# The expert mixture of the last layer: units of four experts in place of units of two, with the banks and buffers laid out for them

## The chip, the cores and the metric

The kernel runs on one core of a Trainium2 chip. Its time is the device time of one execution in microseconds, and the figure for a kernel is the median of several executions. Five engines work in parallel, each through its own instructions in order: TensorE (PE, with its weight loads shown apart as PEld), VectorE (DVE), ScalarE (ACT), GpSimd (POOL) and SyncE (SP). They wait for one another and for DMA transfers through semaphores.

## The reference, cut to what matters

Four transformer layers run one after the other on 1024 rows of 256 numbers. The change lies in the feed-forward part of the last layer, a mixture of 64 experts of which each row uses 8, beside one shared expert:

```python
logits = h @ router_w.T
probs = softmax(logits)
top_vals, top_idx = top_k(probs, 8)
top_vals = top_vals / sum(top_vals)
for e in range(64):                     # each with 64 hidden numbers
    g, u = split(h @ gate_up_proj[e].T, 2)
    out += (silu(g) * u) @ down_proj[e].T * weight_of(row, e)
x = layernorm(x + out + sigmoid(h @ shared_gate) * shared_expert(h))
```

All numbers are float32.

## The kernel before, in words

The stage before the mixture (`attn3`) also routes: it scatters each row, together with its expert numbers, weights and places, into a table in DRAM that has a region of 1024 rows for each expert. The mixture (`ffn3`) then goes through this table in groups of two kinds. An "own" group takes the first 128 rows of each of four consecutive experts. Sixteen such groups cover the 64 experts. A "more" group takes four blocks of 64 rows each, for experts that got more than 128 rows; which experts these are is decided at run time, and ten such groups always run. Further ones run under an `If` at the end only where they are needed; in the profiled execution none ran.

The groups are sorted into one list: own 0, more 0, own 1, own 2, more 1, own 3, more 2, own 4, own 5, more 3, and so on to own 14, own 15, more 9. Each group is cut into two units, so an own unit holds two experts of 128 rows and a more unit two blocks of 64 rows side by side. Every unit goes through these steps (line numbers are those of the profile):

- `load` (per group, on SP): `xr`, the rows from the table (L2414 for own, L2427 for more), and for more groups the experts' weights `few` (L2432). Own groups 1, 3 and 5 first queue 1.5 MB of further expert weights, `gu` and `wd` (L2392, L2396).
- `turn`: PE transposes the rows (L2468), DVE copies them to `xT` (L2470).
- `find` (per group): five small DVE operations (L2446 to L2458) that give `pair`, the row's weight for this expert, and `index`, the row's place in the array of results.
- `hidden`: gate and up products on PE (L2480 own, L2493 more), Silu on ACT (L2486, L2499), and the product of the two on DVE (L2487, L2500).
- `turn_hidden`: PE transposes the hidden numbers (L2507), ACT copies them to `hT` (L2509).
- `down`: PE multiplies by the down weights (L2519, L2532), ACT scales each block of 128 rows into `y` (L2525, L2536), and POOL scatters it to `results` in DRAM with an indirect DMA (L151). An own unit has two scatters, a more unit one. All groups together have 16 x 4 + 10 x 2 = 84.

The order on every engine, SP's queue included, is the one written out by the loop in `run`, with `AHEAD = 2` groups loaded ahead:

```python
for at in range(len(units) + 2):
    if at % 2 == 0 and at // 2 + AHEAD < len(groups):
        load(groups[at // 2 + AHEAD])
    if at + 1 < len(units):
        turn(units[at + 1])
    if at < len(units):
        if at % 2 == 0:
            find(units[at][0])
        hidden(units[at])
    if 0 < at <= len(units):
        turn_hidden(units[at - 1])
    if at > 1:
        down(units[at - 2])
```

So the first `down` stands behind the fourth `turn`. A tile comes out of a pool with a fixed number of buffers; whoever first writes a buffer that is used again waits until all that read it are done, a scatter's DMA among them. The pools of this stage are listed in `SCOPES`. `y` has 5 buffers of two blocks each, and `sel` has 12 for the results of `find`. PSUM has two `wide` tiles of two banks and four single banks. After the mixture, `add_results` loads the results (L2582) when every scatter has landed, adds them up on PE (L2596) and normalises.

Of the kernel before, what the change touches and what calls it, by code (L numbers as in the profile page):

```python
# [29 lines left out]
AF = mybir.ActivationFunctionType  # L30
ALU = mybir.AluOpType
AX = mybir.AxisListType

P = 128
T = 1024
NT = T // P
D = 256
NC = D // P
HALF = 512
# [2243 lines left out]
def shared_expert(k, gate_up, down):  # L2283


    nc = k.nc
    g, u = k.bank(), k.bank()
    for j, ps in enumerate((g, u)):
        for c in range(NC):
            for half in range(2):  # L2290
                nc.tensor.matmul(
                    ps[64 * half : 64 * half + 64, :],
                    lhsT=gate_up[:, c, 64 * j : 64 * j + 64],
                    rhs=k.xcols(c, half * HALF, HALF), start=c == 0, stop=c == NC - 1,
                )
    h = k.tile("shared", [P, HALF])
    nc.scalar.activation(h, g, AF.Silu)
    nc.vector.tensor_tensor(h, h, u, ALU.mult)
    for t in range(4):
        ys = k.wide()  # L2300
        for half in range(2):
            rows = slice(64 * half, 64 * half + 64)
            nc.tensor.matmul(
                ys[:, half * HALF : half * HALF + D], lhsT=h[rows, t * P : (t + 1) * P],
                rhs=down[rows, :], start=True, stop=True,
            )
        for half in range(2):
            at = 4 * half + t
            nc.vector.scalar_tensor_tensor(
                k.x[:, at, :], ys[:, half * HALF : half * HALF + D], k.gate[:, at : at + 1],  # L2310
                k.x[:, at, :], ALU.mult, ALU.add,
            )
# [60 lines left out]
def ffn3(k, a):  # L2373
# [5 lines left out]
    nc = k.nc  # L2379
    shared = k.weights([P, NC, P], a["L3_ffn_shared_gate_up"].rearrange("(c p) f -> p c f", p=P))  # L2380
# [6 lines left out]
    gu = k.tile("gu", [P, 32, 2, NC, P])  # L2387
    wd = k.tile("wd", [P, 32, D])
# [15 lines left out]
    views = dram_disjoint_views(results, E3 + MOST)  # L2404
    regions = k.table.rearrange("(e r) w -> e r w", r=REGION)
    rows, few, xTs, hs, found = {}, {}, {}, {}, {}

    def load(group):
        kind, g = group
        xr = rows[group] = k.tile("xr", [P, 4, ROW])  # L2410
        if kind == "own":
            if g in (1, 3, 5):
                weights_for(20 + 2 * (g - 1))
            nc.sync.dma_start(  # L2414
                out=xr, in_=regions[4 * g : 4 * g + 4, :P, :].rearrange("e p w -> p e w")
            )
            return
        for i in range(2):
            q = 2 * g + i
            _, at = nc.values_load_multi_w_load_instructions(  # L2420
                where[:, q, :], engines=[mybir.EngineType.SP], min_val=0,
                max_val=E3 * REGION - 64,
                skip_runtime_bounds_check_because="both are clamped where they are made",
            )
            few[q] = k.tile("w", [P, 2, 384])
            for h in range(2):
                nc.sync.dma_start(  # L2427
                    out=xr[64 * h : 64 * h + 64, i, :], in_=k.table[bass.ds(at[h], 64), :]
                )
            for h in range(2):  # L2430
                e = at[2 + h].with_bounds(min_val=0, max_val=E3 - 1)
                nc.sync.dma_start(  # L2432
                    out=few[q][:, h, :], in_=a["L3_ffn_few"][:, bass.ds(e * 384, 384)]
                )
# [24 lines left out]
        found[group] = index, pair  # L2459

    def turn(unit):
        (kind, g), i = unit
        n = 2 if kind == "own" else 1
        xr = rows[kind, g][:, n * i : n * i + n, :]
        ps = k.bank()[:, : NC * n * P].rearrange("p (c h n) -> p c h n", c=NC, h=n)
        for c in range(NC):
            for h in range(n):
                nc.tensor.transpose(ps[:, c, h, :], xr[:, h, c * P : (c + 1) * P], k.ident)  # L2468
        xTs[unit] = k.tile("xT", [P, NC, 2, P])
        nc.vector.tensor_copy(xTs[unit][:, :, :n, :], ps)  # L2470

    def hidden(unit):
        (kind, g), i = unit
        xT, ps = xTs.pop(unit), k.bank()
        h = hs[unit] = k.tile("h", [P, 2, 64])
        if kind == "own":
            ps = ps[:, : 2 * P].rearrange("p (h n) -> p h n", h=2)
            for e in range(2):
                for c in range(NC):
                    nc.tensor.matmul(  # L2480
                        ps[:, e, :], lhsT=xT[:, c, e, :], rhs=gu[:, 2 * g + i, e, c, :],
                        start=c == 0, stop=c == NC - 1,
                    )
            gate, up = ps[:, :, :64], ps[:, :, 64:]
            s = k.tile("s", [P, 2, 64])
            nc.scalar.activation(s, gate, AF.Silu)  # L2486
            nc.vector.tensor_tensor(h, s, up, ALU.mult)  # L2487
            return
        ps = ps[:, :P]
        for c in range(NC):  # L2490
            for e in range(2):
                half = slice(64 * e, 64 * e + 64)
                nc.tensor.matmul(  # L2493
                    ps[half, :], lhsT=xT[:, c, 0, half],
                    rhs=few[2 * g + i][:, e, c * P : (c + 1) * P],
                    start=c == 0, stop=c == NC - 1,
                )
        s = k.tile("s", [P, 2, 64])[:, 0, :]
        nc.scalar.activation(s, ps[:, :64], AF.Silu)  # L2499
        nc.vector.tensor_tensor(  # L2500
            h, s.unsqueeze(1).to_broadcast([P, 2, 64]),
            ps[:, 64:].unsqueeze(1).to_broadcast([P, 2, 64]), ALU.mult,
        )

    def turn_hidden(unit):
        ps = k.bank()[:, :P]
        nc.tensor.transpose(ps, hs[unit].rearrange("p h n -> p (h n)"), k.ident)  # L2507
        hs[unit] = k.tile("hT", [P, P])
        nc.scalar.copy(hs[unit], ps)  # L2509

    def down(unit):
        (kind, g), i = unit
        hT, ys, yt = hs.pop(unit), k.wide(), k.tile("y", [P, 2, D])
        index, pair = found[kind, g]
        halves = [slice(64 * h, 64 * h + 64) for h in range(2)]
        ys = ys.rearrange("p (r n) -> p r n", r=2)
        if kind == "own":
            for h, half in enumerate(halves):
                nc.tensor.matmul(  # L2519
                    ys[:, h, :D], lhsT=hT[half, :], rhs=wd[half, 2 * g + i, :],  # L2520
                    start=True, stop=True,
                )
            for h in range(2):
                at = 2 * i + h
                nc.scalar.activation(  # L2525
                    yt[:, h, :], ys[:, h, :D], AF.Copy, scale=pair[:, at, 1:2]
                )
                k.scatter(views, index[:, at : at + 1], yt[:, h, :])
            return
        for r, part in enumerate(halves):  # L2530
            for h, half in enumerate(halves):
                nc.tensor.matmul(  # L2532
                    ys[half, r, :P], lhsT=hT[part, half],
                    rhs=few[2 * g + i][part, h, 2 * P :], start=True, stop=True,
                )
        nc.scalar.activation(  # L2536
            yt[:, 0, :].rearrange("p (r n) -> p r n", r=2), ys[:, :, :P], AF.Copy,
            scale=pair[:, i, 1:2],
        )
        k.scatter(views, index[:, i : i + 1], yt[:, 0, :])  # L2540

    AHEAD = 2

    def run(groups):
        units = [(group, i) for group in groups for i in range(2)]
        for group in groups[:AHEAD]:
            load(group)
        turn(units[0])
        for at in range(len(units) + 2):
            if at % 2 == 0 and at // 2 + AHEAD < len(groups):  # L2550
                load(groups[at // 2 + AHEAD])
            if at + 1 < len(units):
                turn(units[at + 1])
            if at < len(units):
                if at % 2 == 0:
                    find(units[at][0])
                hidden(units[at])
            if 0 < at <= len(units):
                turn_hidden(units[at - 1])
            if at > 1:  # L2560
                down(units[at - 2])

    with k.in_order(transfers=True):
        shared_expert(k, shared, shared_down)
        where, keys, longest = more_blocks(k, ids, column)
        own = [((g + 0.5) / 16, ("own", g)) for g in range(16)]
# [8 lines left out]
def add_results(k, a):  # L2575
# [39 lines left out]
    attn2: dict(wide=3, q=4, k=4, v=2, pt=3, ot=6, tops=2, parts=6),  # L2615
    ffn2: dict(p4=3, t2=8, zero=1),
    attn3: dict(q=12, k=4, v=8, pt=2, p4=2, turned=2, ot=3, t2=4, raw=2),
    ffn3: dict(gu=1, wd=1, route=14, shared=1, xr=4, xT=2, sel=12, s=2, h=2, hT=3, y=5),
    add_results: dict(r=8, z=4),
}  # L2620

# [103 lines left out]
```

## Time and profile before

| | |
|---|---|
| median of 10 executions | 2102.87 us (2098.31 to 2109.95) |
| the profiled execution | 2096.13 us, of which the span is 2094.4 us |
| mean granted TensorE clock | 0.952 |
| busy share of the span | PE 88%, PEld 56%, DVE 64%, ACT 41%, POOL 34% |
| first transposition of the mixture (L2468) | 1932.74 us |
| first and last scatter start (L151, results) | 1941.47 and 2056.83 us |
| scatters | 84, of 0.96 us each on POOL |
| first load of results (L2582) | 2060.60 us |

All times on the profile's axis count from the start of the span. In the list of groups, PE shows two records for one float32 matmul and one for a transposition, so eight records of L2480 are four matmuls. A row of the timeline gives start, duration, engine, line, operation, what is written from what, how many instructions are merged, and in brackets the engine's idle time before it with what ended it.

### The profile page before, as it was taken

The numbers are of one execution on the slowest core, as the hardware profiler recorded it, in microseconds if no ns is written. First come the engines' busy times: TensorE is split into PE (matmuls) and PEld (weight loads), VectorE is DVE, ScalarE is ACT, GpSimd is POOL, SyncE is SP. The second block draws the span as 40 slices with busy tenths as digits, with TensorE's granted clock in tenths as the row PEclk, the third lists the DMA queues.
The fourth block names the chain that finished last, engine by engine and source line by source line (L and its number), as shares of the span: only waits on it lengthen the run. The fifth ranks groups of instructions, "written<-read, shape, count | busy, mean of one in ns | idle before, by whom it ended". The sixth has DMA issues, their size and how long they took to land. (4 is left out here: it accounts for less than half of the span.)

```text
span 2094.4 us, 26185 instructions
## 1 busy us (share of the span) xinstructions
PE 1841.8 (88%) x8163; PEld 1162.8 (56%) x8163; DVE 1332.7 (64%) x2903; ACT 866.8 (41%) x2354; POOL 703.7 (34%) x942
## 2 busy tenths in 40 slices
PE   7988769699999999898889899999999877785896
PEld 4655545456676666576444444445665655554675
DVE  6788846577876665545577354445867676774463
ACT  3666614445253343434444522256444433321451
POOL 5343321333343332231111211115333253533573
PEclk9999979899999999998999999999999999887898
DMA  6322354244444643301330299922443232437985
GB/s 184 85 62 71 82 161 128 80 123 122 132 126 107 175 121 91 82 11 61 93 101 2 101 420 421 422 114 70 98 127 93 66 93 58 122 90 246 333 283 216
DMA packets 180257, 291.91 MB, mean 139 GB/s; under 512 B 36592, under 2 KB 140400, under 8 KB 170896
## 3 DMA queue, kind: packets, MB, share of 16 engines
q1 hardware_dynamic: 153056, 170.46, 29.0%
q0 software_dynamic: 25904, 118.65, 15.0%
q8 instruction: 68, 1.11, 0.2%
q10 hardware_dynamic: 1152, 1.05, 0.1%
q14 instruction: 77, 0.63, 0.1%
HBM read 96.76 MB, written 110.76 MB: 99 GB/s over the span
## 5 line engine op out<-in xcount | busy, mean ns | idle before, releaser
L174 PE MATMUL bank<-xT,w 128*128 128x512 f32 (+1 forms) x960 | 390.1, 546 | 3.9 <-DVE xT L200 2.7
L282 POOL TENSOR_SCALAR p<-p,st 128x128 f32<-128x128 f32 (+7 forms) x256 | 191.7, 749 | 495.3 <-DVE st L281 490.6
L386 DVE STREAM_TRANSPOSE turned<-p 128x128 f32<-128x128 f32 (+7 forms) x232 | 283.5, 1222 | 90.7 <-DMA pt<-turned 48.4
L423 PE MATMUL bank<-pt,v 128*128 128x256 f32 x1216 | 295.1, 388 | 28.2 <-DMA pt<-turned 27.0
L289 PE MATMUL wide<-k,q 128*128 128x512 f32 (+3 forms) x768 | 295.9, 495 | 17.4 <-ACT p L274 16.5
L423 PEld LDWEIGHTS bank<-pt,v 128*128 128x128 f32 x1216 | 237.6, 200 | 85.6 <-issue 37.9
L174 PEld LDWEIGHTS bank<-xT,w 128*128 128x128 f32 x960 | 183.6, 196 | 148.5 <-issue 129.1
L269 DVE TENSOR_REDUCE st<-wide 128x1 f32<-128x128 f32 (+7 forms) x256 | 193.3, 755 | 52.8 <-PE wide L294 46.1
L289 PEld LDWEIGHTS wide<-k,q 128*128 128x128 f32 x768 | 141.0, 192 | 132.0 <-issue 91.0
L274 ACT ACTIVATE p<-wide,st,factor 128x256 f32<-128x256 f32 (+7 forms) x128 | 106.4, 832 | 240.4 <-DVE st L271 129.3
L274 ACT ACTIVATE p<-wide,st 128x128 f32<-128x128 f32 (+7 forms) x128 | 94.9, 741 | 238.9 <-DVE st L269 217.8
L181 PE MATMUL bank<-w,xT 128*128 128x512 f32 (+2 forms) x288 | 115.9, 537 | 5.6 <-DVE xT L2004 4.1
L800 ACT ACTIVATE e<-wide,st 128x128 f32<-128x128 f32 x256 | 90.0, 377 | 73.7 <-DVE st L808 65.0
L264 DVE TENSOR_TENSOR wide<-wide,causal 128x128 f32<-128x128 f32 x192 | 55.9, 291 | 90.1 <-PE wide L289 88.6
L1675 ACT ACTIVATE pt<-wide 128x1024 f32<-128x1024 f32 (+3 forms) x96 | 75.7, 811 | 67.2 <-PE wide L1669 65.4
L151 POOL DMA_INDIRECT results<-y,sel x84 | 80.8, 962 | 52.8 <-ACT y L2525 31.9
L1678 POOL TENSOR_SCALAR_AFFINE_SELECT pt<-pt 128x256 f32<-128x256 f32 x64 | 26.0, 408 | 179.6 <-ACT pt L1675 179.2
L181 PEld LDWEIGHTS bank<-w,xT 128*128 128x128 f32 x288 | 51.7, 193 | 49.3 <-issue 37.3
L1367 POOL DMA_DIRECT2D table<-zero x64 | 34.3, 537 | 132.2 <-DMA table<-zero 132.2
L151 POOL DMA_INDIRECT table<-w x64 | 64.6, 1009 | 36.1 <-issue 14.6
L1627 DVE TENSOR_REDUCE st<-wide 128x2 f32<-128x1024 f32 x64 | 64.3, 1019 | 18.2 <-PE wide L1616 8.9
L866 PE MATMUL bank<-w,ot 128*128 128x256 f32 x256 | 63.7, 394 | 8.2 <-ACT ot L860 5.7
(393 smaller groups left out, 3269.1 us busy)
## 6 DMA issues: line engine op xcount, KB each, us to landing
table<-zero POOLq DMA_DIRECT2D x64, 1120.0 KB
pt<-turned SPq DMA_DIRECT2D x60, 240.0 KB
pt<-turned SPq DMA_DIRECT2D x60, 176.0 KB
pt<-turned SPq DMA_DIRECT2D x156, 64.0 KB
xr<-table SPq DMA_DIRECT2D x16, 560.0 KB
gu<-in_L_ffn_gate_up_dram SPq DMA_DIRECT2D x16, 512.0 KB
r<-results SPq DMA_DIRECT2D x8, 1024.0 KB
w<-in_L_ffn_few_dram SPq DMA_DIRECT2D x40, 192.0 KB
```

The source lines that it names most:

```text
L151: self.nc.gpsimd.indirect_dma_start(out=views.pop(), out_offset=bass.IndirectOffsetOnAxis(ap=index, axis=0), in_=source, in_offset=None,)
L174: self.nc.tensor.matmul(out, lhsT=weight(c), rhs=self.xcols(c, lo, n), start=c == 0, stop=c == NC - 1)
L181: self.nc.tensor.matmul(out, lhsT=self.xcols(c, lo, n), rhs=weight(c), start=c == 0, stop=c == NC - 1)
L269: nc.vector.tensor_reduce(top, scores[:, :n], axis=AX.X, op=ALU.max, negate=True)
L274: nc.scalar.activation(probs[:, :n], scores[:, :n], AF.Exp, bias=top, scale=1.0 if scale is None else scale, accum_out=total,)
L282: self.nc.gpsimd.tensor_scalar(probs[:, :n], probs[:, :n], total, 1.0, ALU.mult, ALU.mult)
L289: self.nc.tensor.matmul(s[:, lo : lo + m], lhsT=query, rhs=key(lo, m), start=True, stop=not masked or lo + m < n, skip_group_check=masked,)
L386: k.nc.vector.transpose(squares.rearrange("p b (k q) -> p b k q", q=32), probs[:, :n].rearrange("p (k i b) -> p b k i", b=4, i=32),)
L423: self.k.nc.tensor.matmul(out.rearrange("p (a q) -> p a q", q=32) if first else out.rearrange("p (s a q) -> p s a q", s=2, q=32), lhsT=val ...
L800: nc.scalar.activation(e[:, r, f, b, :], sc[:, r, f, b, :], AF.Exp, bias=top[:, at : at + 1], accum_out=total[:, at : at + 1],)
L1627: nc.vector.tensor_reduce(st[:, i, :] if half else to, sc[:, :, :n], axis=AX.X, op=ALU.max, negate=True,)
L1675: nc.scalar.activation(two[:, :, lo:], sc[:, :, lo:], AF.Exp)
```

## The change

A unit becomes a whole group: four experts, or two register pairs (four blocks of 64 rows). `turn` writes eight transpositions (four for a more unit) into one `wide` tile and copies it in two instructions. `hidden` computes all four blocks into one bank, followed by one Silu and one product. `turn_hidden` makes two transpositions into one bank and one copy. `down` keeps its matmuls, its scaling and its scatters: four of each of the last two for an own unit, two for a more unit. `AHEAD` becomes 3 and counts units. PSUM gets three `wide` tiles and two single banks. The pools change too, among them `y` to 2 buffers of four blocks and `sel` to 15. The shared expert's hidden tile moves into the pool `y`.

```diff
     def turn(unit):
-        (kind, g), i = unit
-        n = 2 if kind == "own" else 1
-        xr = rows[kind, g][:, n * i : n * i + n, :]
-        ps = k.bank()[:, : NC * n * P].rearrange("p (c h n) -> p c h n", c=NC, h=n)
+        kind, g = unit
+        xr, ps = rows[unit], k.wide()
+        n = 4 if kind == "own" else 2
+        ps = ps[:, : NC * n * P].rearrange("p (c h n) -> p c h n", c=NC, h=n)
         for c in range(NC):
             for h in range(n):
                 nc.tensor.transpose(ps[:, c, h, :], xr[:, h, c * P : (c + 1) * P], k.ident)
-        xTs[unit] = k.tile("xT", [P, NC, 2, P])
-        nc.vector.tensor_copy(xTs[unit][:, :, :n, :], ps)
+        xTs[unit] = k.tile("xT", [P, NC, 4, P])
+        for c in range(NC):
+            nc.vector.tensor_copy(xTs[unit][:, c, :n, :], ps[:, c])
...
     def hidden(unit):
-            ps = ps[:, : 2 * P].rearrange("p (h n) -> p h n", h=2)
-            for e in range(2):
+            ps = ps.rearrange("p (h n) -> p h n", h=4)
+            for e in range(4):
...
     def turn_hidden(unit):
-        ps = k.bank()[:, :P]
-        nc.tensor.transpose(ps, hs[unit].rearrange("p h n -> p (h n)"), k.ident)
-        hs[unit] = k.tile("hT", [P, P])
+        ps, h = k.bank()[:, : 2 * P], hs[unit]
+        for i in range(2):
+            nc.tensor.transpose(
+                ps[:, i * P : (i + 1) * P], h[:, 2 * i : 2 * i + 2, :].rearrange("p h n -> p (h n)"),
+                k.ident,
+            )
+        hs[unit] = k.tile("hT", [P, 2 * P])
         nc.scalar.copy(hs[unit], ps)
...
     def down(unit):
-        hT, ys, yt = hs.pop(unit), k.wide(), k.tile("y", [P, 2, D])
+        hT, ys, yt = hs.pop(unit), k.wide(), k.tile("y", [P, 4, D])
...
+            for i in range(2):
+                for h in range(2):
+                    at = 2 * i + h
+                    nc.scalar.activation(
+                        yt[:, at, :], ys[:, h, i, :], AF.Copy, scale=pair[:, at, 1:2]
+                    )
+                    k.scatter(views, index[:, at : at + 1], yt[:, at, :])
...
-    AHEAD = 2
+    AHEAD = 3
...
-            if at % 2 == 0 and at // 2 + AHEAD < len(groups):
-                load(groups[at // 2 + AHEAD])
+            if at + AHEAD < len(units):
+                load(units[at + AHEAD])
             if at + 1 < len(units):
                 turn(units[at + 1])
             if at < len(units):
-                if at % 2 == 0:
-                    find(units[at][0])
+                find(units[at])
                 hidden(units[at])
...
-    ffn3: dict(gu=1, wd=1, route=14, shared=1, xr=4, xT=2, sel=12, s=2, h=2, hT=3, y=5),
+    ffn3: dict(wide=3, gu=1, wd=1, route=10, xr=4, xT=2, sel=15, s=1, h=2, hT=2, y=2),
```

More of the change, by code (lines that the diff above doesn't have):

```diff
@@ L2295, in shared_expert @@
                 )
-    h = k.tile("shared", [P, HALF])
+    h = k.tile("y", [P, HALF])
     nc.scalar.activation(h, g, AF.Silu)
@@ L2468, in turn @@
                 nc.tensor.transpose(ps[:, c, h, :], xr[:, h, c * P : (c + 1) * P], k.ident)
-        xTs[unit] = k.tile("xT", [P, NC, 2, P])
-        nc.vector.tensor_copy(xTs[unit][:, :, :n, :], ps)
+        xTs[unit] = k.tile("xT", [P, NC, 4, P])
+        for c in range(NC):
+            nc.vector.tensor_copy(xTs[unit][:, c, :n, :], ps[:, c])
     def hidden(unit):
-        (kind, g), i = unit
+        kind, g = unit
         xT, ps = xTs.pop(unit), k.bank()
-        h = hs[unit] = k.tile("h", [P, 2, 64])
+        h = hs[unit] = k.tile("h", [P, 4, 64])
+        s = k.tile("s", [P, 4, 64])
         if kind == "own":
-            ps = ps[:, : 2 * P].rearrange("p (h n) -> p h n", h=2)
-            for e in range(2):
+            ps = ps.rearrange("p (h n) -> p h n", h=4)
+            for e in range(4):
                 for c in range(NC):
                     nc.tensor.matmul(
-                        ps[:, e, :], lhsT=xT[:, c, e, :], rhs=gu[:, 2 * g + i, e, c, :],
+                        ps[:, e, :], lhsT=xT[:, c, e, :],
+                        rhs=gu[:, 2 * g + e // 2, e % 2, c, :],
                         start=c == 0, stop=c == NC - 1,
@@ L2484, in hidden @@
             gate, up = ps[:, :, :64], ps[:, :, 64:]
-            s = k.tile("s", [P, 2, 64])
             nc.scalar.activation(s, gate, AF.Silu)
@@ L2488, in hidden @@
             return
[L2489 to L2499, printed above, removed]
+        ps = ps[:, : 2 * P].rearrange("p (i n) -> p i n", i=2)
@@ new lines, in hidden @@
+        for i in range(2):
+            for c in range(NC):
+                for e in range(2):
+                    half = slice(64 * e, 64 * e + 64)
+                    nc.tensor.matmul(
+                        ps[half, i, :], lhsT=xT[:, c, i, half],
+                        rhs=few[2 * g + i][:, e, c * P : (c + 1) * P],
+                        start=c == 0, stop=c == NC - 1,
+                    )
+        s = s[:, :2, :]
+        nc.scalar.activation(s, ps[:, :, :64], AF.Silu)
+        both = h.rearrange("p (i r) n -> p i r n", i=2)
@@ L2500, in hidden @@
         nc.vector.tensor_tensor(
-            h, s.unsqueeze(1).to_broadcast([P, 2, 64]),
-            ps[:, 64:].unsqueeze(1).to_broadcast([P, 2, 64]), ALU.mult,
+            both, s.unsqueeze(2).to_broadcast([P, 2, 2, 64]),
+            ps[:, :, 64:].unsqueeze(2).to_broadcast([P, 2, 2, 64]), ALU.mult,
         )
     def turn_hidden(unit):
-        ps = k.bank()[:, :P]
-        nc.tensor.transpose(ps, hs[unit].rearrange("p h n -> p (h n)"), k.ident)
-        hs[unit] = k.tile("hT", [P, P])
+        ps, h = k.bank()[:, : 2 * P], hs[unit]
@@ L2509, in turn_hidden @@
+        for i in range(2):
[4 more added lines that the diff above has]
+        hs[unit] = k.tile("hT", [P, 2 * P])
         nc.scalar.copy(hs[unit], ps)
     def down(unit):
-        (kind, g), i = unit
-        hT, ys, yt = hs.pop(unit), k.wide(), k.tile("y", [P, 2, D])
-        index, pair = found[kind, g]
+        kind, g = unit
+        hT, ys, yt = hs.pop(unit), k.wide(), k.tile("y", [P, 4, D])
@@ L2515, in down @@
+        index, pair = found[unit]
         halves = [slice(64 * h, 64 * h + 64) for h in range(2)]
-        ys = ys.rearrange("p (r n) -> p r n", r=2)
         if kind == "own":
[L2518 to L2528, printed above, removed]
-            return
@@ L2530, in down @@
[L2530 to L2540, printed above, removed]
@@ L2542, in ffn3 @@
-    AHEAD = 2
[L2544 to L2547, printed above, removed]
+            ys = ys.rearrange("p (r i n) -> p r i n", r=2, i=2)
+            for i in range(2):
+                for h, half in enumerate(halves):
+                    nc.tensor.matmul(
+                        ys[:, h, i, :], lhsT=hT[half, i * P : (i + 1) * P],
+                        rhs=wd[half, 2 * g + i, :], start=True, stop=True,
+                    )
@@ new lines, in down @@
+            for i in range(2):
+                for h in range(2):
+                    at = 2 * i + h
+                    nc.scalar.activation(
+                        yt[:, at, :], ys[:, h, i, :], AF.Copy, scale=pair[:, at, 1:2]
+                    )
+                    k.scatter(views, index[:, at : at + 1], yt[:, at, :])
+            return
+        ys = ys.rearrange("p (r i n) -> p r i n", r=2, i=4)
+        for i in range(2):
+            for r, part in enumerate(halves):
+                for h, half in enumerate(halves):
+                    nc.tensor.matmul(
+                        ys[half, r, i, :], lhsT=hT[part, i * P + 64 * h : i * P + 64 * h + 64],
+                        rhs=few[2 * g + i][part, h, 2 * P :], start=True, stop=True,
+                    )
+            nc.scalar.activation(
+                yt[:, i, :].rearrange("p (r n) -> p r n", r=2), ys[:, :, i, :], AF.Copy,
+                scale=pair[:, i, 1:2],
+            )
+            k.scatter(views, index[:, i : i + 1], yt[:, i, :])
@@ L2548, in run @@
+    AHEAD = 3
+    def run(units):
+        for unit in units[:AHEAD]:
+            load(unit)
         turn(units[0])
         for at in range(len(units) + 2):
-            if at % 2 == 0 and at // 2 + AHEAD < len(groups):
-                load(groups[at // 2 + AHEAD])
+            if at + AHEAD < len(units):
+                load(units[at + AHEAD])
             if at + 1 < len(units):
```

## The prediction

> **What bounds the kernel now.** I read first the chain that ended last, near its end. A row gives start, duration and what the time went to.
>
> ```profile
> 2047.03 0.66 PE wide L2519 x4
> 2047.71 0.26 ACT y L2525
> ...
> 2055.57 0.96 POOL results L151
> 2056.53 0.30 issue
> 2056.83 3.43 DMA results<-y,sel
> 2060.60 4.80 DMA r<-results
> 2065.45 23.35 PE bank L2596 x100
> ```
>
> From 1952 to 2047 this chain is PE throughout, so it looks as if PE set the pace. But it ends with a row of scatters, and nothing of the next stage can load before the last of them has landed. So I read the timeline of POOL (start, busy time, idle time before) next, and then the end of PE's.
>
> ```profile
> 1941.47 0.96 POOL L151 DMA_INDIRECT results<-y,sel  x1 [17.27 <-ACT y L2525]
> 1942.73 0.96 POOL L151 DMA_INDIRECT results<-y,sel  x1 [0.30 <-issue]
> 1950.62 0.96 POOL L151 DMA_INDIRECT results<-y,sel  x1 [6.93 <-ACT y L2525]
> ...
> 1958.05 0.96 POOL L151 DMA_INDIRECT results<-y,sel  x1 [1.25 <-ACT y L2525]
> 1959.31 0.96 POOL L151 DMA_INDIRECT results<-y,sel  x1 [0.30 <-ACT hT L2509]
> ...
> 1977.35 0.96 POOL L151 DMA_INDIRECT results<-y,sel  x1 [0.62 <-ACT y L2536]
> 1979.55 0.96 POOL L151 DMA_INDIRECT results<-y,sel  x1 [1.24 <-ACT y L2525]
> ...
> 2050.51 0.96 POOL L151 DMA_INDIRECT results<-y,sel  x1 [0.30 <-issue]
> ```
>
> ```profile
> 2048.75 0.45 PE L2532 MATMUL wide<-w,hT 64*64 64x128 f32 x8 [0.46 <-ACT hT L2509]
> ```
>
> A scatter costs 0.96 us, and 0.30 us lie before each, whatever the row names as the cause. From 1958.05 (the seventh) to 2056.83 (the last) are 77 steps in 98.78 us. Two of them hold a real wait, 0.32 and 0.94 us beyond the 0.30; the rest is (98.78 - 1.26) / 77 = 1.266 us a step. When PE is done at 2049.2, POOL still has six scatters to start, over 7 us of work. POOL is thus the bound of this stage from 1950 on, with PE close behind it. 84 scatters need 84 x 1.266 = 106.3 us, and the change keeps all 84. The end of the stage after is therefore the start of the first scatter, plus 106.3, plus whatever POOL waits.
>
> **What is removed or merged.** The number of matmuls and transpositions is the same. For two units ACT has two Silu of 0.28 and two copies of 0.26, and gets one of each over twice the columns (the 128x256 rows of ACT are 0.38 to 0.47); DVE has two products of 0.28 and gets one, by its 128x256 rows about 0.42. That is a tenth or two of a us per group on each. PE changes from one kind of matmul to the next half as often: four transpositions take 0.59 and two 0.37, so a start costs some 0.15. All of this lies beside POOL's row of scatters and I cost it at nothing. Without that cover it would be worth what the second rival says.
>
> **The first scatter.** In step `at` the order is the transpositions of unit at+1, `find` and `hidden` of at, `turn_hidden` of at-1, `down` of at-2. So the first `down` still stands behind the fourth `turn`, but that is now the fourth group (own 2) and no longer the second half of the second. Before, two scatters went out at 1941; now none can until own 1 and own 2 are there. Own 1 comes behind 1.5 MB of weights that its `load` queues first, on SP's queue in the same order as before, and PE waits for it:
>
> ```profile
> 1946.12 1.09 PE L2468 MATMUL bank<-ident,xr 128*128 128x128 f32 x4 [5.45 <-DMA xr<-table]
> 1947.14 1.12 PE L2493 MATMUL bank<-w,xT 128*64 128x128 f32 x8
> 1948.19 0.48 PE L2507 MATMUL bank<-ident,h 128*128 128x128 f32 x1
> ...
> 1952.61 0.45 PE L2532 MATMUL wide<-w,hT 64*64 64x128 f32 x8
> ```
>
> After this idle time PE works at half pace until 1952.6 (eight records of L2493 1.05 us here, 0.59 later), then at full pace. With the durations of these rows the new order gives: eight transpositions 2.1 (to 1948.2), sixteen records of `hidden` for more 0 2.1 (1950.3), two transpositions of hidden numbers 0.6 (1950.9), eight transpositions of own 2, mostly at half pace, 2.0 (1952.9), sixteen records of `hidden` for own 1 at 0.11, 1.8 (1954.7), two transpositions 0.35 (1955.0), eight records of `down` 1.26 (1956.3), then 0.1 and 0.47 for the first `y` and 0.28 to POOL. The first scatter starts at about 1957.1. Own 2's rows are queued right behind own 1's, and PE did not wait for them at 1952.99 before; if they land only then, the start is 2 us later. From 1957.1 without a further wait the row would end at 1957.1 + 106.3 = 2063.4, against 2056.83 + 1.27 = 2058.1 before: **+5.3 us**.
>
> **The new wait: two buffers of y.** In the changed program the first `y` of unit u writes the buffer of unit u-2 and waits until all its scatters have landed; before, five buffers reached back five units, and no `y` waited for that. So I need the time L from a scatter's start to its landing. The last one, with idle DMA, shows 3.43 us in the chain above. While the queues are full, three `find` that waited for the last scatter of a group four back show it:
>
> ```profile
> 1968.78 0.19 DVE L2454 TENSOR_REDUCE sel<-sel 128x4 f32<-128x32 f32 x1 [0.76 <-DMA results<-y,sel]
> 2002.41 0.19 DVE L2454 TENSOR_REDUCE sel<-sel 128x4 f32<-128x32 f32 x1 [0.80 <-DMA results<-y,sel]
> 2026.17 0.22 DVE L2454 TENSOR_REDUCE sel<-sel 128x8 f32<-128x64 f32 x1 [0.41 <-DMA results<-y,sel]
> ```
>
> Those scatters started at 1961.85, 1996.01 and 2021.34, so L was 6.9, 6.3 and 4.8 us. The `find` that did not wait bound it from above: under 5.0 at 2006.09, 4.5 at 2033.43, 3.9 at 2045.50. I take 4.7, between these, and keep 3.4 and 6.3 as ends.
>
> After its landing, the scatter of unit u can start 0.1 + 0.47 + 0.28 = 0.85 us later. POOL meanwhile works on unit u-1. If that is an own unit, it is busy 1.27 + 4 x 1.266 = 6.33 us from the start of the last scatter of u-2, longer than 4.7 + 0.85. If it is a more unit, only 1.27 + 2 x 1.266 = 3.80 us. Then POOL idles L + 0.85 - 3.80 = L - 2.95 = 1.75 us. There are nine own units behind a more unit: 9 x 1.75 = **+15.8 us** (4.3 by L = 3.4, 30 by 6.3).
>
> The wait also holds up what stands behind it on ACT: the Silu of u+3 and the copy of u+2, with DVE's product and PE's `hidden` behind them. From the `y`, PE needs about 5.3 us for the rest of a `down`, four, then sixteen records, two transpositions and the next eight; with that the next own unit's scatter falls at L - 2.95 to L - 2.4 as well, so it adds at most 0.5 a gap, which I leave to the range. The 15 buffers of `sel` make `find` wait for scatters five units back: no later than the `y` in question, so nothing. SP's loads wait for `turn` and `find` of the unit four before, both ahead of POOL. The old wait for own 5's rows (PE idle to 1974.5, POOL short by 1.26 us at 1977 to 1979) goes under: POOL reaches that unit only after 1979.
>
> A rule to weigh here: the Trainium skill, "DMA: Bandwidth & Descriptors", section "Anatomy of one DMA — SWDGE (gpsimd) path", gives such a DMA about 2.0 us plus its bytes at 436 GB/s, an estimate of 2.3 us for 128 KB. By it no own unit would ever wait on two buffers and the sum would be +5.3 alone; the landings above say 3.4 to 6.9, and I go by them.
>
> **The sum.** 5.3 + 15.8 = +21 us on the profiled execution, 2096.1 to 2117. That execution lies 6.7 below the median of 2102.87, so the median after is 2124.
>
> **The rivals.**
> (a) No gaps: landings near 3 us, or ACT far enough ahead. Only the late start remains, +5.3, with 2 us of play: 2106 to 2111. For it speaks 3.43; against it the three waits above.
> (b) Faster: PE is the bound, as the chain of waits says. Halving the starts saves 26 units x 2 starts x 0.15 = 7.8 us: 2095. It decides only if POOL has no queue left when PE ends, and it has six scatters; and it must win back the late start.
> (c) Worse: landings near 7 us throughout, as the first of the three, because every unit now sends its scatters in one burst into full queues. Nine gaps of 4.05 are 36, with the start 42: 2145. It decides from L = 6.3 on; against it speak the `find` under 5.0.
>
> **How the numbers follow.** A measurement can tell about 0.2% (4.2 us) from no change. The forecast (gaps of 0.5 to 3.3 us) has 0.72, (a) 0.13, (b) 0.03, (c) 0.12. The range goes from the forecast with L = 3.4 (+10) to that with 6.3 (+36), and a little into both sides: 2110 to 2140. Faster 0.03; same is the lower edge of (a), 0.05; slower 0.92.
>
> **What would show it.** After: first scatter of results near 1957; a POOL idle time of 1 to 3 us, released by `y`, before the first scatter of each own unit behind a more unit; ACT's first `y` of these units waiting for the DMA of results; PE no longer full from 1975 to 2045; the last scatter near 2078. Wrong: scatters at 1.27 us all through, a first scatter before 1953, or steps other than 1.27 within a unit.

## The result, and the profile after

| | before | after |
|---|---|---|
| median | 2102.7 us (2093.5 to 2110.0, 46 executions) | 2126.99 us (2116.4 to 2130.1, 13 executions) |
| the profiled execution, its span | 2096.13, 2094.4 us | 2125.49, 2123.8 us |
| mean granted TensorE clock | 0.952 | 0.947 |
| first transposition of own 1 (L2468) | 1946.12 us | 1947.46 us |
| first and last scatter start (L151) | 1941.47 and 2056.83 us | 1956.85 and 2085.25 us |

The changed kernel is slower: ratio 1.0108 [1.0096, 1.012], some 24 us between the medians. The two profiled executions lie 29.4 us apart, because that of before lay 6.6 us below its median and that of after 1.5 below; a single profile is good for a few us only.

First the timeline of POOL after, at places where the row of scatters starts, breaks and ends (the bracket holds POOL's idle time before the scatter; 0.30 is the usual step).

```profile
1956.85 0.96 POOL L151 DMA_INDIRECT results<-y,sel  x1 [29.65 <-ACT y L2535]
...
1967.88 0.96 POOL L151 DMA_INDIRECT results<-y,sel  x1 [3.73 <-ACT y L2535]
...
1985.48 0.96 POOL L151 DMA_INDIRECT results<-y,sel  x1 [5.24 <-ACT y L2535]
...
2051.44 0.96 POOL L151 DMA_INDIRECT results<-y,sel  x1 [4.22 <-ACT y L2535]
...
2085.25 0.97 POOL L151 DMA_INDIRECT results<-y,sel  x1 [0.30 <-issue]
```

Between the gaps a step is 1.266 us as before, so 83 steps from the first scatter to the last are 105.1 us, and the rest of the 128.4 us is gaps: 23.3 us in nine of them. Eight stand before the first scatter of an own unit behind a more unit: own 1 (3.43 beyond the 0.30), own 3 (4.93), own 4 (0.78), own 6 (2.19), own 8 (2.45), own 9 (2.45), own 11 (3.90), own 12 (2.16). Own 14, the last such unit, has none. The ninth gap, 1.00, is that of more 6. Before, such gaps came to 1.26 us from the seventh scatter on (the two real waits of the prediction).

That gives the account of the last scatter, which starts 28.4 us later than before: 1.3 us because own 1's rows came later in this execution; 5.1 us of start (own 1's first transposition to the first scatter is 9.4 us, against 4.3 to where an unbroken row would have begun before: 1958.05 less six steps of 1.266, less 1946.12); and 22.0 us of gaps (23.3 less 1.26). The sum is 28.4.

The windows say what the other engines did meanwhile. First after, then before: a stretch, its length, busy time (instructions) of PE, PEld, DVE, ACT and POOL, granted clock, DMA share, GB/s.

```profile
1975.00:1985.00 10.00, 7.24 (x46) 6.36 (x47) 2.58 (x8) 1.87 (x5) 4.01 (x5) 0.66 0.61 211
2035.00:2045.00 10.00, 2.27 (x32) 1.52 (x34) 2.70 (x9) 2.67 (x8) 6.76 (x8) 0.79 0.76 256
```

```profile
1975.00:1985.00 10.00, 10.00 (x87) 7.08 (x86) 5.83 (x20) 5.56 (x18) 6.61 (x8) 1.00 1.00 346
2035.00:2045.00 10.00, 10.00 (x93) 7.53 (x91) 6.16 (x21) 5.48 (x18) 7.60 (x8) 1.00 0.48 164
```

PE, full before, now stands for a quarter of the first stretch and most of the second, and its granted clock falls to 0.66 and 0.79. So the list of waits of the stage (1930 to 2120: us in total, times, longest):

```profile
PE wide L2544 <- ACT y L2548: 30.5, 10, 7.7
ACT y L2548 <- DMA results<-y,sel: 22.0, 6, 7.0
ACT y L2535 <- DMA results<-y,sel: 10.8, 6, 4.2
```

Read upwards, ACT waits for the landing of scatters, as foretold, but twice as long at the more units' `y` (L2548) as at the own units' (L2535). And PE waits for that `y` of the more units, longer than for anything else: 30.5 us. The prediction's list of signs names no such wait. One case shows how it works, more 6 and own 11: ACT first, then PE.

```profile
2044.22 0.47 ACT L2548 ACTIVATE y<-wide,sel 128x256 f32<-128x256 f32 x1 [6.97 <-DMA results<-y,sel]
...
2050.69 1.57 ACT L2535 ACTIVATE y<-wide,sel 128x256 f32<-128x256 f32 x4 [0.65 <-PE wide L2528]
```

```profile
2034.08 1.09 PE L2468 MATMUL wide<-ident,xr 128*128 128x128 f32 x8
...
2036.64 0.45 PE L2544 MATMUL wide<-w,hT 64*64 64x128 f32 x8
2044.74 0.70 PE L2544 MATMUL wide<-w,hT 64*64 64x128 f32 x8 [7.65 <-ACT y L2548]
2045.38 1.97 PE L2468 MATMUL wide<-ident,xr 128*128 128x128 f32 x8
2047.14 2.22 PE L2482 MATMUL bank<-gu,xT 128*128 128x128 f32 x16
...
2049.51 1.14 PE L2528 MATMUL wide<-wd,hT 64*128 64x256 f32 x8
```

`down` of a more unit is a loop over its two blocks, and in it the matmuls of the second block come after the scaling of the first, on the same `wide` tile. PE does the first half at 2036.64 and then waits for the first `y`, which waits until the scatter that started at 2037.63 has landed, 6.6 us later. From that `y` on, PE does the second half, the next unit's transpositions, a `hidden`, a `turn_hidden` and own 11's `down`, before own 11's `y` can start at 2050.69. Much of this is at half pace, because PE has stood for 7.65 us: eight transpositions take 1.97 in place of 1.09.

So a gap of POOL can have two causes: the own unit's `y` waits for a landing itself, or it waits for its matmuls, which PE does late because the more unit's `y` ahead of it waited. ACT's rows tell them apart, here for own 1 and own 3:

```profile
1967.13 1.57 ACT L2535 ACTIVATE y<-wide,sel 128x256 f32<-128x256 f32 x4 [4.24 <-DMA results<-y,sel]
...
1984.73 1.57 ACT L2535 ACTIVATE y<-wide,sel 128x256 f32<-128x256 f32 x4 [0.65 <-PE wide L2528]
```

Own 1 and own 4 are of the first kind, and so is own 9 (its row names PE, but its matmuls had ended 2.6 us before it started). Own 3, 6, 8 and 11 are of the second kind, 13.5 of the 23.3 us. More 6 waits for a landing. Own 12's `y` does too, but its scatter starts 2.23 us after the start of the first `y`, where the others take 0.75; what the 1.5 us more are was not found.

### The profile page after: what moved, and what is told of

It is laid out like the page before. It is cut to its first block, busy times and chain, and to the rows that moved or that the text cites. A ratio compares the mean times of both kernels' runs of the same rounds, so it can differ in the third digit from the quotient of the medians.

```text
span 2123.8 us, 26017 instructions
## 1 busy us (share of the span) xinstructions
PE 1841.9 (87%) x8163; PEld 1171.5 (55%) x8163; DVE 1328.0 (63%) x2877; ACT 857.7 (40%) x2302; POOL 703.7 (33%) x942
## 3 DMA queue, kind: packets, MB, share of 16 engines
q0 software_dynamic: 25904, 118.65, 14.8%
## 5 line engine op out<-in xcount | busy, mean ns | idle before, releaser
L151 POOL DMA_INDIRECT results<-y,sel x84 | 80.7, 961 | 78.3 <-ACT y L2535 56.2
L151 POOL DMA_INDIRECT table<-w x64 | 64.6, 1009 | 36.0 <-issue 19.9
L255 DVE TENSOR_TENSOR x<-bank,x 128x256 f32<-128x256 f32 x112 | 44.4, 404 | 44.0 <-PE bank L877 16.7
```

The costliest lines, as they stand in the source:

```text
L151: self.nc.gpsimd.indirect_dma_start(out=views.pop(), out_offset=bass.IndirectOffsetOnAxis(ap=index, axis=0), in_=source, in_offset=None,)
```

## The experiments

The kernels of one set ran on one chip with the kernel before among them, and the sets on different chips. On the chip of the first four below, before takes 2105.4 us, close to the 2102.7 of the result. On the chips of the other two sets it takes 2141.8 and 2143.2 us. So times are compared within a set only, as ratios to before.

**Two suspects, alone and together.** The theories: the landing (two buffers of `y` reach back too short a way) or the place of PE's second half behind the more unit's first `y`. Four kernels take them apart. The first is the changed kernel again.

> The changed kernel as it is, beside its variants on one chip, since the four variants ran on a chip on which the kernel before needs 2141.8 us and not 2102.7. All theories: a ratio of 1.008 to 1.013 to the kernel before. If it is below 1.003, the change costs nothing on that chip, and the ratios of the variants have to be read against that.

The second keeps the two buffers, and moves the more unit's matmuls ahead of both its scalings:

```diff
         for i in range(2):
             for r, part in enumerate(halves):
...
                         rhs=few[2 * g + i][part, h, 2 * P :], start=True, stop=True,
                     )
+        for i in range(2):
             nc.scalar.activation(
```

> Matmuls of a more unit's down ahead of its two scalings, again, beside the changed kernel on the same chip. If PE held behind a more unit's first y is what makes the gaps (theory A1, as the ratio of 1.0012 says): at least 10 us below the changed kernel, and no idle time of PE before the down of more units that a y ends. If the ratio of 1.0012 came from the other chip: within 5 us of the changed kernel.

The third cuts `y` into tiles of two blocks, in the same memory (four of two in place of two of four). An own unit takes two of them, a more unit one, so that a more unit no longer holds four blocks' room for two blocks:

```diff
-        hT, ys, yt = hs.pop(unit), k.wide(), k.tile("y", [P, 4, D])
+        hT, ys = hs.pop(unit), k.wide()
...
             for i in range(2):
+                yt = k.tile("y", [P, 2, D])
                 for h in range(2):
...
+        yt = k.tile("y", [P, 2, D])
         ys = ys.rearrange("p (r i n) -> p r i n", r=2, i=4)
...
-    ffn3: dict(wide=3, gu=1, wd=1, route=10, xr=4, xT=2, sel=15, s=1, h=2, hT=2, y=2),
+    ffn3: dict(wide=3, gu=1, wd=1, route=10, xr=4, xT=2, sel=15, s=1, h=2, hT=2, y=4),
```

> The four tiles of y again, beside the changed kernel. If the wait of y for landings is the main cause (theory A): 10 us or more below the changed kernel, gaps of POOL under 8 us in all. If the wait is only the occasion and PE held behind y is the cause (theory A1): the more unit's y still stops PE between its two halves, the time is 0 to 8 us below the changed kernel.

The fourth has both edits.

> Four tiles of y and the matmuls first. Neither the landing two units back nor a y holds PE: theory A and A1 together leave the late first scatter alone, 2 to 7 us above the kernel before. If a third cause is in the deeper units (rival B): still 10 us or more above.

| kernel | median us | ratio to before | start us | gaps of POOL us | own 1's first transposition to last scatter us |
|---|---|---|---|---|---|
| before (profile of the result) | 2105.42 | 1 | 4.3 | 1.3 | 110.7 |
| changed kernel | 2128.86 | 1.0111 [1.008, 1.0143] | 9.0 | 22.3 | 136.4 |
| matmuls first | 2117.41 | 1.0063 [1.0041, 1.0085] | 9.1 | 15.2 | 129.3 |
| pairs | 2115.63 | 1.0051 [1.0033, 1.007] | 10.1 | 5.8 | 120.8 |
| both | 2108.29 | 1.0022 [1.0004, 1.004] | 9.0 | 3.4 | 117.5 |

Start is the time from own 1's first transposition to the first scatter (for before, to where an unbroken row would have begun). In each row start, 105.1 us of steps and gaps make up the last column (to 0.2). The ratios are not exactly those of the medians: for both, the medians lie 2.9 us apart and the ratio says 4.6. The order of the times is that of the gaps, but the profiled executions were not all near their medians: those of the changed kernel and of matmuls first took 3.3 and 5.9 us more than these, that of the kernel before 6.6 us less than its own. So the steps between rows are read from the medians too.

The waits of the stage, in the same view as above, for matmuls first:

```profile
ACT y L2535 <- DMA results<-y,sel: 28.3, 10, 6.0
ACT y L2549 <- DMA results<-y,sel: 26.5, 6, 7.2
```

for pairs:

```profile
PE wide L2546 <- ACT y L2550: 14.8, 9, 6.3
...
ACT y L2536 <- DMA results<-y,sel: 9.7, 9, 1.8
...
ACT y L2550 <- DMA results<-y,sel: 2.9, 3, 1.7
```

and for both:

```profile
ACT y L2536 <- DMA results<-y,sel: 20.6, 15, 2.2
...
ACT y L2551 <- DMA results<-y,sel: 4.8, 4, 2.1
```

With the matmuls first, ACT waits 54.8 us for landings, against 32.8 in the changed kernel, and yet the kernel is 11 us faster. PE's second half no longer stands behind that wait. What is left, 15.2 us of gaps in this profile, stands at `y` that wait for a landing, all but 1.5 us at own 12 (the same late scatter as above); by the medians the buffers are worth 9.1 us here (2117.41 less 2108.29). With pairs, ACT's waits for landings shrink to 12.6 us, the place of the second half still costs PE 14.8 us, and POOL's gaps fall to 5.8. Of these, 5.4 are a single gap at own 3. There PE was held twice, 2.1 us by the more unit's `y` and 2.6 by the rows of own 5, which are queued behind a block of weights. With both edits only one gap of over half a us is left, at own 1, and PE's wait behind it is again one for rows (2.8 us, own 3's, likewise behind weights). So both suspects are guilty, and about equally: by the medians the second half's place is worth 11.5 us where the two buffers of four blocks stay (2128.86 to 2117.41) and 7.3 where `y` comes in pairs (2115.63 to 2108.29), and the buffers 13.2 and 9.1. They overlap by some 4 us, as they would if the same wait feeds both, though that much is within the noise of so few executions (the changed kernel has four). Together they make 20.6 of the 23.4 us by which the changed kernel is slower on this chip. The 2.9 us that remain fit the late start, of which neither edit takes anything away; that they are the start is argued, not shown.

And this is the last of the mixture's matmuls in both:

```profile
2054.67 0.67 PE L2546 MATMUL wide<-w,hT 64*64 64x128 f32 x16 [1.55 <-ACT hT L2517]
```

Its last scatter starts at 2068.49, 13.2 us after these matmuls end; before, 7.6 us lay between the two. PE is further ahead of POOL than it was: what merging saves on PE lengthens POOL's queue and not the row of scatters.

**The same edits on the chip where before takes 2141.8 us.** This set had run first.

> The changed kernel with two buffers of y as they are, but in a more unit's down all sixteen records of PE stand ahead of the two scalings, as in an own unit's. PE then no longer stands behind a y that waits for a landing. Theory A1 (the part of the 23 us above the 15.8 forecast comes from PE: held behind a more unit's first y, it has a down, a turn, a hidden and the next down to do only after the landing, partly at half pace): gaps fall to about L - 2.95 each, 14 to 18 in all, and the median to 2117 to 2123. Theory A2 (landings alone are longer than the 4.7 us taken): the gaps stay near 23 us, and the time at 2124 to 2129.

> The changed kernel with the same 8 KB of y, but cut into four tiles of two blocks: an own unit takes two, a more unit one. Theory A (the gaps are the wait of y for the landing two units back): an own unit's third block behind a more unit then waits for scatters that began 2.5 us earlier, with POOL 6.3 us busy since, so no gap up to landings of about 8 us. The 23 us of gaps go, the late start stays: the median is 2105 to 2110, and the first scatter still begins near 1957. Rival B (the gaps come from the deeper units: fewer units in flight, rows loaded too late, PE idle and at half pace): nothing in it depends on y, and the time stays at 2122 to 2130.

Matmuls first measured 1.0012 [0.9995, 1.0029], pairs 1.0077 [1.0052, 1.0102]: the order of the two is the reverse. For pairs the interval overlaps that of the other chip; it is matmuls first that measures less here. The changed kernel was not run in this set, so what either edit gains on this chip is not known. The waits of pairs (1920 to 2130) show what else goes on here:

```profile
PE wide L2546 <- ACT y L2550: 31.8, 8, 7.3
ACT y L2550 <- remote: 14.4, 5, 4.0
...
ACT y L2550 <- DMA results<-y,sel: 1.2, 1, 1.2
```

The wait that the view puts down to landings is 1.2 us at this `y`. But ACT stops at the same `y` for 14.4 us with a releaser that is none of this core's engines (remote; whether a landing hides in it, the view doesn't say), and PE's second half waits for this `y`, 31.8 us. In all, stops of this kind come to 26.6 us of this stage here, 47.8 in matmuls first, and 21.0 in the kernel before with fewer buffers, below; in the profiles of before, after and the four kernels above there are none. One from matmuls first, on ACT and then PE:

```profile
2009.29 0.89 ACT L2549 ACTIVATE y<-wide,sel 128x256 f32<-128x256 f32 x2
2016.79 0.28 ACT L2502 ACTIVATE s<-bank 128x128 f32<-128x128 f32 x1 [6.61 <-remote]
```

```profile
2009.49 1.09 PE L2496 MATMUL bank<-w,xT 128*64 128x128 f32 x16 [0.18 <-issue]
```

PE had the Silu's input ready at 2010.58, and ACT took it up at 2016.79. Such stops stand in every profile of these two chips, and POOL's row has more gaps there: 41 us even in the kernel before with three buffers, against 10.3, counted from the first scatter as well, in the profile of before. How much of them the stops make was not worked out. A start that is some us earlier or later, or a `y` that waits, can be hidden in there. The kernels that follow must be read so.

**The start.** Draining the first unit ahead of own 1's transpositions, on top of pairs, same set:

```diff
+            early = at == 1
-            if at + 1 < len(units):
+            if at + 1 < len(units) and not early:
                 turn(units[at + 1])
...
-            if at > 1:
+            if early:
+                down(units[0])
+                turn(units[2])
+            if at > 2:
                 down(units[at - 2])
```

> As pairs, and the first unit's turn_hidden and down are put ahead of the turn that waits for own 1's rows. If the late first scatter costs 5 us (theory), four scatters go out between 1946 and 1952, the next ones are set by PE's refill after 1946, and the time is 2 to 6 us below pairs: 2100 to 2106. If the late start costs nothing because the row of scatters fills up later anyway (rival), it equals pairs within 2 us.

Measured 1.0059 [1.0033, 1.0085], 2156.74 us against 2156.68 of pairs, not the 2 to 6 us less that were expected. The first scatter starts at 1960.72 in place of 1965.74, and the time does not follow (nor can a few us be told apart here). In another set, the kernel with both edits, its first two units drained ahead of own 1's transpositions by the same means:

> As both (four tiles of y, matmuls first), and the first two units are brought to their scatters before the turn that waits for own 1's rows. If the rest of 3 to 5 us is the late first scatter (theory): six scatters leave before own 1 is through, POOL then waits for PE's refill, and the time is 2 to 6 us below both, at a ratio of 0.998 to 1.001. If the late start is not what is left (rival): as both, 1.002 to 1.003.

Measured 1.0008 [0.9993, 1.0023], which can't be told from before. Since both was not in that set, this doesn't show what the early start gave. The same edit in the kernel before (its first four units):

> The kernel before, units of two, with its first four units brought to their scatters before the turn that waits for own 1's rows. Six scatters leave in the idle time of PE up to 1946 in place of two; POOL's steady row then starts about 2 us earlier. Theory (POOL sets the end): 1 to 4 us faster than the kernel before, 0.998 to 0.9995. If PE set the end: no change, 0.9995 to 1.0005.

Measured 0.9981 [0.9961, 1.0002]. It is the only kernel that may beat before, and the interval doesn't settle it.

A pipeline shorter by one step, `turn_hidden` in the step of its own `hidden`, on top of that kernel with both edits:

> As both_early, and the pipeline of units is one step shorter: hidden of a unit, turn of the next, turn_hidden of the same unit, down of the one before. After own 1's rows the first down then needs one step less, some 3 to 4 us; PE stalls a little for the product in each step, which POOL's row covers as long as it has a queue. Theory: 1 to 4 us below both_early, a ratio of 0.996 to 0.999, better than both kernels. If PE's stalls come out on POOL: 1.000 to 1.005.

Measured 1.006 [1.0034, 1.0085], the slowest of its set: a miss. PE's `turn_hidden` now waits 33.8 us in all for the product of its own unit (L2512 behind L2489), a wait that is not in the list of the kernel it was built on.

**Fewer buffers in the kernel before.** `y` from 5 to 3, nothing else, in both of these sets:

> The kernel before with 3 buffers of y in place of 5, units unchanged: y then waits for the landing three units back, the reach in blocks that the changed kernel has. Theory A: a unit behind two more units finds POOL busy for only 1.27 + 2 x 1.266 = 3.8 us since the scatter in question began, so about nine gaps of L - 2.95, 1 to 3 us each, at the own units behind more groups, as in the changed kernel and without its late start: 2113 to 2125. Rival B (units of four are the cause): 2100 to 2106, as before.

> The kernel before with 3 buffers of y again, as the chip of its first run stopped engines for other reasons too. Theory A alone (every y that waits for a landing costs a gap): 1.004 to 1.010. Theory A1 (the wait costs little as long as PE and ACT have other units to go on with, and no down holds PE behind a y in units of two): 1.000 to 1.004.

Measured 1.0005 [0.999, 1.002] and 1.0006 [0.999, 1.0023]. ACT's `y` waits 1.2 and 3.1 us for landings in the two profiles, so the edit made next to no wait here, and POOL had 41 and 43 us of gaps that could take it in. It doesn't show what three buffers would cost where before takes 2105.

## Why the prediction was right

**POOL is the bound: right.** The step stayed at 1.266 us, the end of the stage is the last scatter, and both, whose row is almost unbroken, ends with it while PE has been done for 13 us. The second rival, PE as the bound, fell on the condition that the prediction set it: POOL still has a queue when PE ends (before, it was seven scatters at 2049.2, not the six of the working). In the changed kernel itself the gaps hand part of the time to PE, as said above.

**The first scatter: right in its place, by luck: two errors cancelled.** Forecast 1957.1, measured 1956.85. But own 1's rows came 1.3 us later than in the profile of before, and PE took 9.4 us from there, not the 11.0 of the working, since it was back at full pace from about 1951.5, sooner than assumed. The start's +5.3 was 5.1 in the trace (1956.85 in place of 1957.1). In time, both is 2.9 us over before by the medians [0.8 to 8.4 us by the interval of its ratio], which allows it; no run takes the start alone away on a chip that would show it.

**The landing: right in kind; its size is found only where PE is not held.** Nine gaps of L - 2.95 with L = 4.7 were 15.8 us, with 4.3 as the lower end. With the matmuls first, 15.2 are found in the profile, and 9.1 by the medians. In the changed kernel, gaps at which the waiting `y` itself stood behind a landing come to 8.3 us (own 1, 4, 9, more 6, and 0.7 at own 12). The other 15 are PE's chain, 13.5, and the 1.5 at own 12. That the median came out within 3 us of the 2124 forecast is thus in part luck: the landing's own term was little more than half of what was forecast, and the chain that the sum left out made up for it. The landings themselves were not all near 4.7 either: their median over the 84 scatters is 3.7 in the profile of after, and where a `y` waited L went from 2.5 to 6.6. (The prediction's second L, from 1996.01 to 2002.41, is 6.4 and not 6.3, which changes nothing.) The estimate by the Trainium skill's "DMA: Bandwidth & Descriptors", "Anatomy of one DMA — SWDGE (gpsimd) path", 2.3 us, would have given no gap. The rows speak against it while loads are under way: 6.6 us for the scatter of 2037.63. Near the end of the stage it comes close: from 2067 on, three `y` waited for landings of 2.5 us; the last scatter shows 4.25.

**The step that was mis-sized** is the one on what stands behind the waiting `y`: "it adds at most 0.5 a gap, which I leave to the range". It had the chain right, down to the rest of a `down`, but priced it with PE at full pace and with L = 4.7. From the start of a more unit's `y` to the next own unit's first scatter the working makes a path of 5.3 us on PE and some 0.75 from there to POOL, 6.05. POOL has six scatters and one more step to cover it, 7 x 1.266 = 8.86, so that chain's gap is L + path - 8.86, an account of the same times and not a test of them. At more 6 and own 11 L was 6.6 and the path 7.22 (2044.22 to 2051.44): 4.95, and the two gaps found are 1.00 + 3.90. At more 1 and own 3 L was 5.56 (1971.68 to the `y` at 1977.24) and the path 8.24 (to 1985.48): 4.94, and 4.93 was found. Half pace alone lengthens the PE work of these two paths by 1.4 us (0.25 + 0.88 + 0.27, by rows of 0.70, 1.97 and 2.22 against 0.45, 1.09 and 1.95 at full pace) and 2.4 us (0.25 + 0.88 + 1.29, with its `hidden` at 3.24):

```profile
1980.16 3.24 PE L2482 MATMUL bank<-gu,xT 128*128 128x128 f32 x16
```

So this chain added 1.3 and 2.3 us to the landing's L - 2.95 there, not 0.5, and in all some 7 us of gaps (22.3 against 15.2), or 7 to 11 us by the medians, against the 4.5 that nine times 0.5 allowed.

The Trainium skill, "TensorE: Matmul & The Clock Gate", Part 1, says that PE falls to half clock after some 3.4 us without work and needs about as long at work to come back. The rows of the two long waits agree: after 6.15 and 7.65 us of standing it is at half pace, and back at full pace within 3 to 5 us. Shorter waits are not so regular: in the changed kernel eight transpositions took 1.97 us after a wait of 2.53 us (before 2016.86), in matmuls first 1.06 after one of 2.88 (before 1979.86). By the skill's rule a wait of 7 us in front of PE costs an estimated 1.7 us on top, which the working left out.

**Against the list of what would show it.** The first scatter came near 1957. The idle times released by `y` stand at own units behind more units, eight of nine, and are wider than 1 to 3 us (0.8 to 4.9). ACT does wait for the DMA of results, but longer at the more units, and at four of the eight own units with a gap what released `y` was PE and not the DMA. PE is not full from 1975 to 2045. The last scatter started at 2085.25, not near 2078: the gaps were 7.5 us more than forecast (23.3 against 15.8), the start 0.25 early.

**The rivals.** No gaps, with only the late start left (2106 to 2111), is what both is, at 2108.29: a rival that was right about the price of the start and wrong about the buffers. Landings near 7 us throughout did not come about: where a `y` waited they are 2.5 to 6.6 us in the changed kernel, and at the own units with a gap in matmuls first 3.8 to 6.0, with a mean of 4.8.

## What to carry to other kernels

When units are merged and the memory stays the same, count a pool's buffers in time and not in units: the reach must cover issue, landing and the queue of the engine that sets the pace, and small tiles in the same memory reach further than large ones that are half empty. When a wait is new, walk down what stands behind it on every engine, and price that walk with PE at half pace and at the longest landing seen; a matmul that stands behind the scaling out of its own tile hands every stop of ACT on to PE. Ahead of an engine that is already behind, saving instructions buys only queue.

## What the runs showed of the hardware

The same kernel took different times on different chips. Before takes 2103 to 2105 us in the result and in the set of the four kernels, and 2142 to 2143 on the two other chips, 1.8% more. On the latter the profiles show ACT and DVE stopped for up to 9.0 us at a time with nothing on the core that releases them, 18 to 62 us in all of this stage; on the former there are none. What these stops are was not found: the wait names only "remote", and no profile of before or after exists on those chips. On one of them the order of two edits (matmuls first and pairs) was the other way round; that the stops did it is not shown.

An indirect scatter of 128 KB landed after a median of 3.7 us in the changed kernel (4.8 in both), after 2.5 to 6.6 us where a `y` waited for it, and after 3.43 (before) and 4.25 us (after) for the last one. More 6 alone, at 6.6, held PE for 7.65 us: what a wait costs is set by the long landings, not by the middle one.
